# A two-layer MetaFormer on one core: padding cleared alone, qkv weights in thirds, ten convolution rows on VectorE, two dispatch steps a tap

## The chip, the cores and the metric

The kernel runs on one core of a Trainium2 chip, all in float32. The core has five instruction streams that run beside each other and meet only at semaphores: TensorE for matrix products (PE in the profile; PEld is its loading of weights), VectorE (DVE), ScalarE (ACT), GpSimd (POOL) and SyncE (SP, which here only starts transfers). Products land in PSUM banks, and another engine has to evict them. The metric is the device time of one execution in microseconds (us); lower is better. Before the change the median of three runs is 3289.18 us (3285.77 to 3293.74).

## The reference

The input is x with 4 images of 384 channels on 32x32 pixels. Two layers follow each other, each of the form "x plus mixer of norm(x), then plus feed-forward of norm(x)":

```python
# layer 0
x = x + conv0(ln_c(x))     # attention over the 1024 pixels, 8 heads of 48, with clipped relative
                           # tables for query, key and value; then a projection with bias
t = t + ffn0(ln_t(t))      # 384 -> 1536 -> 384, both weights Kronecker products, exact gelu
# layer 1
x = x + conv1(ln_c(x))     # depthwise 7x7 + 5x3 + 3x5 + (1x7 then 7x1) + (1x5 then 5x1) + bias
t = t + ffn1(ln_t(t))      # 4 experts of 384 -> 1536 -> 384, the best 2 of each token, weighted
```

ln_c and ln_t subtract the mean over channels and divide by the standard deviation. The depthwise kernels are summed into one 7x7 kernel, which fits since all are centered: 49 taps per channel.

## The kernel before

The work runs in three phases.

`qkv_phase` computes queries, keys and values for 8 tiles of 512 tokens. Channels lie on partitions in KC = 3 chunks of 128. For a tile, `token_stats` transposes the tokens (`row_ps`, line 75), takes mean and variance on VectorE (`s_st`, `s_mv`), and a square root on ScalarE gives `rstd`. The mean is not subtracted from x; instead `center` takes from the weight `wq` its mean over input channels (matmuls with a matrix of ones, `sum_ps`, line 116, then three VectorE operations on `wq` per 384 columns, line 118). `to_partitions` spreads `rstd` over partitions (`s_dg`, `all_ps`, lines 103 and 105). Six products `qk_ps` of three matmuls each follow (line 163), scaled by VectorE into `qk_sb`, then four `v_ps` products, scaled by ScalarE into `va` (line 177). `va` holds each head's 48 value columns padded to VW = 64; the padding must be zero, and line 135 clears the whole tile on GpSimd. That clearing stands on GpSimd's stream after the first half of `make_identity` (a clearing of `ident`) and ahead of its second half (the select that writes the diagonal). SP loads the first x tile, then `wq` in three row blocks of 576 KB, then the next two x tiles.

`attention_phase` handles the 8 heads in an order written out by hand. The change does not touch it.

`rest_phase` does everything after attention, image by image. `front(b)` is the attention's projection (`proj_ps`, line 903, its sum into the residual `xb` at line 906) and the whole first feed-forward; `normalise(b)` prepares the convolution, `image(b)` writes the padded picture `img`, `convolve(b)` runs the taps, and `dispatch(b)` is gates (`gate_ps`, `logits_ps`, eight transposed tiles `row_ps`, which VectorE takes for statistics and ScalarE copies into `rows`), then positions and expert block lists on VectorE (`pos`, `slot`, `row`) and 16 scatters of token rows into `xs_d` on GpSimd (line 1103). All of these are generators: a `yield` ends a step and gives an estimate of what the step costs VectorE and PE.

The expert part runs in 67 blocks of 128 tokens, in four groups of 13, 16, 16 and 22; group b needs the scatters of images up to b. In `blocks` each block gathers its tokens (`xg`, line 1147, GpSimd), transposes them (`xT_ps`, line 1160), and makes twelve times three `e_ps` matmuls (line 1198), a gelu on ScalarE and one `y_ps` matmul (line 1176). Weights come by indirect DMA on GpSimd (line 1166), three half blocks ahead; where the expert stays the same, the transfer moves nothing. `yo` (line 1179) evicts a block's sum on VectorE. After every twelfth of a block `more` adds 1.36 to PE's clock of estimates and takes steps from `others()` until VectorE's clock of estimates has caught up. So the remaining convolutions, fronts and dispatches are woven into the blocks by these estimates. At a group's end a loop, whatever the clocks say, takes steps until the next group's scatters are issued:

```python
for i, g in enumerate(groups):
    blocks(g, lambda k: more(g, k))
    if i + 1 < len(groups):
        while "after" not in groups[i + 1]:
            next(todo)
```

Image 0's convolution comes before all blocks, in `first()`, and is split between two engines. VectorE takes all of chunk 0 and the first `own` = 4 rows of chunk 1, one `scalar_tensor_tensor` per tap and part (line 993). PE takes the rest by `taps_by_matmul`: chunk 2 in two parts of 16 rows and chunk 1's other 28 rows in two parts of 14, with diagonal weights in 64x64 quarters (`tap_ps`, line 1037), even and odd taps in two halves that ScalarE copies out (`taps`, line 1047) and one more matmul adds up (`taps_ps`, line 1048, a single bank). VectorE then adds the part to `xb` (line 1051). `taps_by_matmul` is a generator too, with 27 steps a part: 25 pairs of taps, the sum, the add. `first()` takes three of its steps after each tap of VectorE.

Within an engine's stream the Tile framework may move instructions by its own priorities; instructions wrapped in `tc.keep_in_program_order` keep their order among each other.

Of the kernel before, what the change touches and what calls it, by code (L numbers as in the profile page):

```python
# [13 lines left out]
ALU = mybir.AluOpType  # L14
# [4 lines left out]
P = 128  # L19
# [101 lines left out]
def qkv_phase(tc, cst, x, w_qkv, qk_d, v_d, xs_d):  # L121

    nc = tc.nc
    one, ident = cst["one"], cst["ident"]
    with ExitStack() as es:
        wp = es.enter_context(tc.tile_pool(name="q_w", bufs=1))
        work = es.enter_context(tc.tile_pool(name="q_work", bufs=2))  # L130
        ev = es.enter_context(tc.tile_pool(name="q_ev", bufs=4))
        psum = es.enter_context(tc.tile_pool(name="q_ps", bufs=3, space=PSUM))
        psmm = es.enter_context(tc.tile_pool(name="q_mm", bufs=4, space=PSUM))
        va = wp.tile([P, HEADS, B * NBLK, VW], F32, name="va")
        nc.gpsimd.memset(va, 0.0)
        zero = wp.tile([P, 1, C], F32, name="zero")
        nc.gpsimd.memset(zero, 0.0)
        wq = wp.tile([P, KC, 3 * C], F32, name="wq")
        xts = {}

        def load(t):
            b, n0 = divmod(t * TOK, N)
            xts[t] = work.tile([P, KC, TOK], F32, tag="xt", name="xt", bufs=3)
            nc.sync.dma_start(xts[t], x[b, :, n0 : n0 + TOK].rearrange("(k p) n -> p k n", p=P))

        load(0)
        for k in range(KC):
            nc.sync.dma_start(wq[:, k, :], w_qkv[k * P : (k + 1) * P, :])
        stats = result(token_stats(nc, (work, psum, "st"), ident, xts[0], cst["eps6"]))
        center(nc, psum, "st", one, wq)  # L150
        for t in range(NT // TOK):
            b, n0 = divmod(t * TOK, N)
            xt = xts.pop(t)
            _, rstd = stats
            ps = to_partitions(nc, (work, psum, "st"), ident, one, rstd)
            scale = work.tile([P, TOK], F32, tag="scale", name="scale")
            nc.scalar.copy(scale, ps)
            if t + 1 < NT // TOK:
                load(t + 1)
            for m in range(2 * KC):  # L160
                ps = psmm.tile([P, TOK], F32, tag="mm", name="qk_ps")
                for k in range(KC):
                    nc.tensor.matmul(  # L163
                        ps, wq[:, k, m * P : (m + 1) * P], xt[:, k, :], start=(k == 0), stop=(k == KC - 1)
                    )
                sb = ev.tile([P, TOK], F32, tag="qk", name="qk_sb")
                nc.vector.tensor_tensor(sb, ps, scale, ALU.mult)
                nc.gpsimd.dma_start(qk_d[m * P : (m + 1) * P, t * TOK : (t + 1) * TOK], sb)
            if t + 1 < NT // TOK:
                stats = result(token_stats(nc, (work, psum, "st"), ident, xts[t + 1], cst["eps6"]))  # L170
            for j in range(TOK // P):
                ps = psmm.tile([P, TOK], F32, tag="mm", name="v_ps")
                for k in range(KC):
                    nc.tensor.matmul(
                        ps[:, :C], xt[:, k, j * P : (j + 1) * P], wq[:, k, 2 * C :], start=(k == 0), stop=(k == KC - 1)
                    )
                nc.scalar.activation(  # L177
                    va[:, :, t * (TOK // P) + j, :HD], ps[:, :C].rearrange("p (h d) -> p h d", d=HD),
                    AF.Copy, scale=rstd[:, j, :],
                )  # L180
            w = NBLK // 2 * VW
            nc.gpsimd.dma_start(
                v_d.rearrange("h p n -> p h n")[:, :, t * w : (t + 1) * w],
                va[:, :, t * NBLK // 2 : (t + 1) * NBLK // 2, :].rearrange("p h c d -> p h (c d)"),
            )
            if 2 <= t < 2 + NEXP:
                rows = xs_d[(t - 2) * CAP : (t - 1) * CAP].rearrange("(n p) c -> p n c", p=P)
                n = rows.shape[1] // 2
                for r in (rows[:, :n], rows[:, n:]):
                    tc.keep_in_program_order(nc.gpsimd.dma_start(r, bcast(zero, 1, r.shape[1])))  # L190
# [644 lines left out]
def rest_phase(tc, cst, x, ao_d, ins, xs_d, y_d, x2_d, out):  # L835
# [9 lines left out]
    with ExitStack() as es:  # L845
# [138 lines left out]
        def convolve(b, xb, parts):  # L984


            for k in range(KC):
                nc.vector.tensor_scalar_add(xb[:, k, :], xb[:, k, :], cbias[:, k : k + 1])
            acc = xb.rearrange("p k (y x) -> p k y x", x=IMG)
            for dy in range(7):  # L990
                for dx in range(7):
                    for k, y0, y1 in parts:
                        nc.vector.scalar_tensor_tensor(  # L993
                            acc[:, k, y0:y1], img[:, k, dy + y0 : dy + y1, dx : dx + IMG],
                            w7[:, k, dy, dx : dx + 1], acc[:, k, y0:y1], ALU.mult, ALU.add,
                        )

                    if b:
                        tc.keep_in_program_order(nc.vector.memset(pause, 0.0))
                    yield sum(0.12 + 0.0337 * (y1 - y0) for _, y0, y1 in parts) + 0.06, 0.0  # L1000
            if b + 1 < B:
                nc.sync.dma_start(x2_d[:, b * N : (b + 1) * N].rearrange("(k p) n -> p k n", p=P), xb)
# [10 lines left out]
        def taps_by_matmul(xb, parts):  # L1013

            def diagonals(k, w):
                d = w[:, : 49 * 64].rearrange("p (t m) -> p t m", m=64)
                nc.gpsimd.tensor_tensor(
                    d, bcast(half.unsqueeze(1), 1, 49),  # L1020
                    bcast(w7[:, k].rearrange("p y x -> p (y x)").unsqueeze(2), 2, 64), ALU.mult,
                )
                return d

            half = small.tile([P, 64], F32, tag="half", name="half", bufs=1)
            nc.vector.tensor_tensor(half, ident[:, :64], ident[:, 64:], ALU.add)
            diag = {k: diagonals(k, w) for k, w in zip(dict.fromkeys(k for k, *_ in parts), wts[1])}
            yield
            for k, y0, ny in parts:
                n = ny * IMG  # L1030
                sums = [ps_y.tile([P, TOK], F32, tag="y", name="tap_ps", bufs=2) for _ in range(2)]
                for t0 in range(0, 49, 2):
                    for t in range(t0, min(t0 + 2, 49)):
                        dy, dx = divmod(t, 7)
                        for h in range(2):
                            lo = 64 * h
                            nc.tensor.matmul(
                                sums[h][64 * (t % 2) : 64 * (t % 2) + 64, :n].rearrange("p (y x) -> p y x", x=IMG),
                                diag[k][lo : lo + 64, t, :],
                                img[lo : lo + 64, k, dy + y0 : dy + y0 + ny, dx : dx + IMG],  # L1040
                                start=(t < 2), stop=(t > 46),
                            )
                    yield
                po = ps_y.tile([P, TOK], F32, tag="t", name="taps_ps")
                for h in range(2):
                    e = hid.tile([P, TOK], F32, tag="hs", name="taps", bufs=HS)
                    nc.scalar.copy(e[:, :n], sums[h][:, :n])
                    nc.tensor.matmul(po[64 * h : 64 * h + 64, :n], half, e[:, :n], start=True, stop=True)
                yield
                acc = xb[:, k, y0 * IMG : y0 * IMG + n]  # L1050
                nc.vector.tensor_tensor(acc, acc, po[:, :n], ALU.add)
                yield

        def new(shape, name, dt=F32):
# [226 lines left out]
        def first():  # L1281


            half, own = IMG // 2, 4
            rest = (IMG - own) // 2
            taps = taps_by_matmul(
                xbs[0], [(2, 0, half), (2, half, half), (1, own, rest), (1, own + rest, rest)]
# [2 lines left out]
            halves = []  # L1290
            yield from normalise(xbs[0], halves)
            yield from image(halves)
            for _ in convolve(0, xbs[0], [(0, 0, IMG), (1, 0, own)]):
                for _ in range(3):
                    next(taps, None)
                yield
            for _ in taps:
# [3 lines left out]
        def others():  # L1301
# [11 lines left out]
            for b in range(1, B):  # L1313
# [2 lines left out]
                halves = []  # L1316
                later = ahead(b + 1, halves)
                for t, cost in enumerate(convolve(b, xbs[b], [(k, 0, IMG) for k in range(KC)])):
                    for start, steps in ((2, side), (12, later)):
                        more = next(steps, None) if t >= start else None  # L1320
                        if more:
                            cost = cost[0] + more[0], cost[1] + more[1]
                    yield cost
# [150 lines left out]
```

## Time and profile before

| what | us |
|---|---|
| median of 3 runs | 3289.18 |
| profiled execution | 3284.5 |
| its span, first to last instruction | 3282.7 |
| PE busy | 2986.8 (91%) |
| VectorE busy | 1991.4 (61%) |
| first PE instruction | 15.02 |
| image 0's convolution, first tap matmul to last add | 1752.4 to 1859.0 |
| first expert matmul | about 1938 |
| last convolution tap | about 2596 |
| last expert block's transposes | 3232.7 |

Times in the timeline are counted from the span's start. A timeline line reads: start, duration, engine, source line, operation, output <- input, shapes, how many instructions were merged, and in square brackets how long the engine stood idle before and what released it. A line of a stretch gives the window, its length, then the busy time (and the number of instructions) of PE, PEld, DVE, ACT and POOL, the clock that PE was granted (1.00 is full), the share of the DMA engines and GB/s. A float32 matmul leaves two records.

### The profile page before, as it was taken

To read this page: it belongs to the slowest core of one execution; us is meant where nothing else is said; L and a number is where in the kernel's file an instruction comes from. 1 tells how busy PE (TensorE), PEld (TensorE's weight loads), DVE (VectorE), ACT (ScalarE), POOL (GpSimd) and SP (SyncE) were. 2 spreads that over 40 slices of the span, in tenths; PEclk is the share of its full clock that TensorE was granted. 3 is DMA by queue.
4 is the path that set the end of the run, shared out by engine and by line. 5 is a ranking of instruction groups with operands and counts; after the bars stand their busy time and mean duration, and the time that the engine had idled before them with its cause. 6 is when DMAs were issued, how large, how long until landed. Compare 5 with 4: busy or idle time off the path is not lost.

```text
span 3282.7 us, 64040 instructions
## 1 busy us (share of the span) xinstructions
PE 2986.8 (91%) x25591; PEld 2063.8 (63%) x25591; DVE 1991.4 (61%) x3619; ACT 1331.7 (41%) x2687; POOL 1159.6 (35%) x1100
## 2 busy tenths in 40 slices
PE   8998998989898989999879888998999999999996
PEld 4445666666675656666643445575577777777775
DVE  2227777768676877777748659998999730001101
ACT  1115656555555655565511131342443333233322
POOL 2225536263536364544520032123125231114422
PEclk9999999999999999999989998998999999999998
DMA  3786464545455555646240313261156035474852
GB/s 140 268 300 195 102 194 115 179 122 174 117 174 129 169 136 141 171 120 187 74 153 23 113 66 142 80 257 56 44 209 234 27 115 213 152 277 151 303 208 70
DMA packets 222202, 500.60 MB, mean 152 GB/s; under 512 B 92192, under 2 KB 145056, under 8 KB 214224
## 3 DMA queue, kind: packets, MB, share of 16 engines
q1 hardware_dynamic: 156720, 214.75, 21.4%
q0 software_dynamic: 43552, 228.24, 18.8%
q10 hardware_dynamic: 21632, 53.52, 6.4%
q8 instruction: 202, 3.31, 0.4%
q14 instruction: 96, 0.79, 0.1%
HBM read 543.58 MB, written 152.37 MB: 212 GB/s over the span
## 4 chain that ended last, share of the span: by engine, by line
PE 65%; DVE 12%; issue 8%; ACT 7%; DMA 5%; POOL 3%; SPq 1%; another core or an unknown queue 0%; ACTq 0%; POOLq 0%; DVEq 0%
PE e_ps L1198 14%; PE y_ps L1176 13%; DVE xb L993 7%; PE av_ps L215 6%; PE t_ps L406 6%; PE tabq_ps L215 5%; PE sc_ps L215 4%; PE tv_ps L215 3%; ACT arow L387 3%; PE tabk_ps L215 2%; PE qk_ps L163 2%; ACT aT L407 2%; PE a_ps L416 2%; DVE oT L470 2%; DMA qs<-qk_d 1%
## 5 line engine op out<-in xcount | busy, mean ns | idle before, releaser
L349 POOL TENSOR_TENSOR bias<-b,s 128x416 f32<-128x416 f32 (+24 forms) x656 | 660.0, 1043 | 631.8 <-DMA s<-sd 424.5
L1198 PEld LDWEIGHTS e_ps<-xT,w 128*128 128x128 f32 x4824 | 654.6, 192 | 230.5 <-issue 16.7
L1198 PE MATMUL e_ps<-xT,w 128*128 128x128 f32 x4824 | 672.6, 277 | 20.2 <-DVE xb L906 8.0
L1176 PE MATMUL y_ps<-w,eh 128*128 128x384 f32 x1608 | 652.5, 490 | 17.7 <-ACT eh L1201 14.3
L993 DVE SCALAR_TENSOR_TENSOR xb<-img,c_w,xb 128x1024 f32<-128x1024 f32 (+1 forms) x539 | 611.0, 1196 | 0.0
L1201 ACT ACTIVATE eh<-e_ps,w 128x128 f32<-128x128 f32 x804 | 293.3, 367 | 753.8 <-PE e_ps L1198 692.3
L1166 POOL DMA_INDIRECT w<-in_w,row x134 | 164.0, 1224 | 786.4 <-PE y_ps L1176 270.7
L377 DVE CUSTOM_DVE_ANT_0 arow<-sc_ps,bias 128x1024 f32<-128x1024 f32 x256 | 312.8, 1222 | 191.4 <-POOL bias L349 101.9
L398 DVE TENSOR_REDUCE extra<-arow 128x32 f32<-128x32 f32 (+24 forms) x768 | 378.7, 551 | 30.2 <-ACT arow L387 30.2
L406 PEld LDWEIGHTS t_ps<-ident,arow 128*128 128x128 f32 x2048 | 226.4, 144 | 265.0 <-ACT arow L387 185.3
L407 ACT COPY aT<-t_ps 128x512 f32<-128x512 f32 x512 | 275.5, 589 | 267.4 <-PE t_ps L406 241.9
L387 ACT ACTIVATE arow<-arow,nm 128x1024 f32<-128x1024 f32 x256 | 297.0, 1160 | 177.6 <-DVE nm L377 166.5
L406 PE MATMUL t_ps<-ident,arow 128*128 128x128 f32 x2048 | 289.1, 286 | 74.4 <-ACT arow L387 73.3
L215 PE MATMUL sc_ps<-kk,qs 48*32 48x512 f32 x4096 | 294.0, 625 | 50.8 <-DMA qs<-qk_d 26.8
L1179 DVE TENSOR_TENSOR yo<-y_ps,w 128x384 f32<-128x384 f32 x67 | 37.2, 556 | 446.9 <-PE y_ps L1176 439.7
L1176 PEld LDWEIGHTS y_ps<-w,eh 128*128 128x128 f32 x1608 | 248.0, 193 | 31.1 <-ACT eh L1201 16.9
L215 PEld LDWEIGHTS av_ps<-aT,vb 128*64 128x64 f32 x4096 | 222.3, 137 | 52.3 <-ACT aT L407 37.8
L303 DVE STREAM_TRANSPOSE b<-tabk_ps 128x480 f32<-128x480 f32 x256 | 219.1, 1000 | 44.5 <-PE tabk_ps L215 24.8
L215 PE MATMUL av_ps<-aT,vb 128*64 128x128 f32 x4096 | 237.7, 274 | 0.0
L215 PE MATMUL tabk_ps<-tab,kq 48*128 48x480 f32 x512 | 225.7, 588 | 3.3 <-DVE b L303 3.3
L215 PE MATMUL tabq_ps<-tab,kq 48*128 48x480 f32 x512 | 224.5, 585 | 0.7 <-ACT va L177 0.7
L308 ACT COPY st<-tabq_ps 128x480 f32<-128x480 f32 x256 | 141.8, 561 | 75.3 <-PE tabk_ps L215 36.5
(212 smaller groups left out, 3190.4 us busy)
## 6 DMA issues: line engine op xcount, KB each, us to landing
sd<-st SPq DMA_DIRECT2D x128, 480.0 KB
s<-sd SPq DMA_DIRECT2D x512, 120.0 KB
xs_d<-zero POOLq DMA_DIRECT2D x8, 3072.0 KB
tvw<-in_tv ACTq DMA_DIRECT2D x120, 192.0 KB
y_d<-yo SPq DMA_DIRECT2D x67, 192.0 KB
qk_d<-qk_sb POOLq DMA_DIRECT2D x48, 256.0 KB
qs<-qk_d SPq DMA_DIRECT2D x256, 48.0 KB
kq<-qk_d ACTq DMA_DIRECT2D x56, 192.0 KB
```

The lines of the kernel that those rows point to most:

```text
L215: ins = nc.tensor.matmul(*args, **kw)
L303: turn = nc.vector.transpose(b2.rearrange("p e y x -> p x (e y)")[:, i + j], ps[:, j, : SPAN * IMG])
L349: nc.gpsimd.tensor_tensor(bias[:, y0:y1, :], bass.AP(b2.tensor, b2.offset + (e * IMG + y0) * IMG, [list(b2.ap[0]), [(step * IMG + 1) * IMG ...
L377: nc.vector.tensor_tensor_reduce(s["flat"], ps.rearrange("p h n -> p (h n)"), s["bias"].rearrange("p y x -> p (y x)"), -SCALE, BIG, ALU.ad ...
L387: nc.scalar.activation(s["flat"], s["flat"], AF.Exp, bias=s["nm"], scale=-1.0, accum_out=dn[:, y % YT : y % YT + 1])
L398: pin(nc.vector.tensor_reduce(ex[:, i, :], a[:, p0:p1, :].rearrange("p y x -> p x y"), AX.X, ALU.add))
L406: pin(nc.tensor.transpose(pt[:, j, :], s["flat"][:, k0 : k0 + P], ident))
L407: pin(nc.scalar.copy(aT[:, 4 * g : 4 * g + 4, s["y"] % YB, :], pt))
L993: nc.vector.scalar_tensor_tensor(acc[:, k, y0:y1], img[:, k, dy + y0 : dy + y1, dx : dx + IMG], w7[:, k, dy, dx : dx + 1], acc[:, k, y0:y1 ...
L1176: nc.tensor.matmul(py, hs, w[:, o : o + C], start=(ff == 0), stop=(ff == NF - 1))
L1198: nc.tensor.matmul(ph, w[:, o : o + P], xT[k][:, c, :], start=(c == 0), stop=(c == KC - 1))
L1201: nc.scalar.activation(hs, ph, AF.Gelu, bias=w[:, o : o + 1])
```

## The change

There are three separate edits.

At the start, only the padding columns of `va` are cleared, on VectorE. `wq` is loaded in nine pieces of 192 KB, first the query third of all three row blocks, then the key third, then the value third; and each third is centered right before its first use: the query third before product 0, the key third before product 3 and the value third before the first `v_ps`, all in tile 0.

In image 0's convolution VectorE takes ten rows of chunk 1 instead of four, and PE two parts of 11 rows instead of 14. The taps of image 0 and the adds of line 1051 are kept in program order. The 108 steps of `taps_by_matmul` are spread over the taps from the third to the last, the rest at the last, so an add stands after every twelfth tap or so: after taps 13, 25, 37 and 48 (counted from 0).

In `others()` each tap of images 2 and 3 takes two steps of the dispatch of the image before, instead of one, from the third tap on; the next image's front still joins with one step per tap from the thirteenth.

```diff
         va = wp.tile([P, HEADS, B * NBLK, VW], F32, name="va")
-        nc.gpsimd.memset(va, 0.0)
+        nc.vector.memset(va[:, :, :, HD:], 0.0)
...
         load(0)
-        for k in range(KC):
-            nc.sync.dma_start(wq[:, k, :], w_qkv[k * P : (k + 1) * P, :])
+
+        for i in range(3):
+            for k in range(KC):
+                own = slice(i * C, (i + 1) * C)
+                nc.sync.dma_start(wq[:, k, own], w_qkv[k * P : (k + 1) * P, own])
         stats = result(token_stats(nc, (work, psum, "st"), ident, xts[0], cst["eps6"]))
-        center(nc, psum, "st", one, wq)
...
             for m in range(2 * KC):
+                if t == 0 and m % KC == 0:
+                    center(nc, psum, "st", one, wq[:, :, m * P : m * P + C])
...
+            if t == 0:
+                center(nc, psum, "st", one, wq[:, :, 2 * C :])
             for j in range(TOK // P):
...
                     for k, y0, y1 in parts:
-                        nc.vector.scalar_tensor_tensor(
+                        tap = nc.vector.scalar_tensor_tensor(
                             acc[:, k, y0:y1], img[:, k, dy + y0 : dy + y1, dx : dx + IMG],
                             w7[:, k, dy, dx : dx + 1], acc[:, k, y0:y1], ALU.mult, ALU.add,
                         )
+                        if b == 0:
+                            tc.keep_in_program_order(tap)
...
                 acc = xb[:, k, y0 * IMG : y0 * IMG + n]
-                nc.vector.tensor_tensor(acc, acc, po[:, :n], ALU.add)
+                tc.keep_in_program_order(nc.vector.tensor_tensor(acc, acc, po[:, :n], ALU.add))
...
-            half, own = IMG // 2, 4
+            half, own = IMG // 2, 10
...
-            for _ in convolve(0, xbs[0], [(0, 0, IMG), (1, 0, own)]):
-                for _ in range(3):
+
+            steps = 4 * 27
+            for t, _ in enumerate(convolve(0, xbs[0], [(0, 0, IMG), (1, 0, own)])):
+                for _ in range(steps if t == 48 else max(0, t - 1) * steps // 48 - max(0, t - 2) * steps // 48):
                     next(taps, None)
                 yield
...
-                    for start, steps in ((2, side), (12, later)):
+                    for start, steps in ((2, side), (2, side), (12, later)):
                         more = next(steps, None) if t >= start else None
```

## The prediction

> **What bounds the kernel now.** I read the page first, then the stretches of 50 us, then the timeline where TensorE (PE) is not full, and the chain of waits there. The page:
>
> ```profile
> PE 2986.8 (91%) x25591; PEld 2063.8 (63%) x25591; DVE 1991.4 (61%) x3619; ACT 1331.7 (41%) x2687; POOL 1159.6 (35%) x1100
> PE 65%; DVE 12%; issue 8%; ACT 7%; DMA 5%; POOL 3%; SPq 1%; another core or an unknown queue 0%; ACTq 0%; POOLq 0%; DVEq 0%
> ```
>
> PE is busy 91% of the span and carries 65% of the chain that ended last, so a change pays where it takes away idle time of PE, or work that PE stands behind. The stretches (busy us of PE, PEld, DVE, ACT, POOL, then PE clock):
>
> ```profile
> 1800.00:1850.00 50.00, 41.87 (x380) 18.78 (x376) 33.39 (x47) 2.04 (x4) 0.00 (x0) 0.90 0.14 52
> 2000.00:2050.00 50.00, 34.56 (x127) 21.37 (x126) 47.08 (x63) 7.26 (x15) 7.44 (x4) 0.76 0.44 166
> 2250.00:2300.00 50.00, 35.76 (x148) 22.44 (x147) 41.64 (x62) 11.64 (x21) 19.71 (x17) 0.83 0.15 49
> 2700.00:2750.00 50.00, 50.00 (x311) 39.97 (x310) 1.67 (x3) 15.04 (x40) 9.40 (x10) 1.00 0.65 239
> ```
>
> From 2700 on PE is full: there every microsecond won earlier reaches the end. The change touches three places with holes: the start, image 0's convolution (1752 to 1859), and the border between block groups 0 and 1 (2245 to 2300). At the start (timeline):
>
> ```profile
> 0.89 13.76 POOL L135 MEMSET va<- 128x16384 f32 x1
> 14.69 0.28 POOL masks.py:199 TENSOR_SCALAR_AFFINE_SELECT ident<-ident 128x128 f32<-128x128 f32 x1
> 15.02 2.82 PE L75 MATMUL row_ps<-ident,xt 128*128 128x128 f32 x12 [15.02 <-POOL ident masks.py:199]
> 17.64 6.87 PE L116 MATMUL sum_ps<-wq,one 128*128 128x384 f32 x18
> 25.20 15.61 PE L163 MATMUL qk_ps<-xt,wq 128*128 128x512 f32 x36
> ```
>
> PE's first instruction waits 15.02 us for the identity, which stands behind the va memset on POOL. In image 0's convolution:
>
> ```profile
> 1806.20 19.31 PE L1037 MATMUL tap_ps<-img,w 64*64 64x448 f32 x196
> 1832.91 1.76 PE L1048 MATMUL taps_ps<-taps,half 128*64 128x448 f32 x4 [7.41 <-DVE xb L1051]
> 1834.60 21.34 PE L1037 MATMUL tap_ps<-img,w 64*64 64x448 f32 x196
> 1858.33 0.62 DVE L1051 TENSOR_TENSOR xb<-xb,taps_ps 128x448 f32<-128x448 f32 x1 [22.99 <-PE taps_ps L1048]
> ```
>
> PE ends last; VectorE (DVE) then idles 23 us. Besides, PE waits 7.4 us for an add that stands late in DVE's stream, and its next 20 tap matmuls run at half pace. At the group border:
>
> ```profile
> 2236.86 1.02 POOL L1103 DMA_INDIRECT xs_d<-rows,pos  x1 [21.77 <-DVE b_first L782]
> 2261.81 1.02 POOL L1147 DMA_INDIRECT xg<-xs_d,slot  x1 [1.01 <-DMA xs_d<-rows,pos]
> 2265.04 0.88 PE L1160 MATMUL xT_ps<-ident,xg 128*128 128x128 f32 x3 [7.52 <-DMA xg<-xs_d,slot]
> ```
>
> Group 1's first gather waits for the 16 scatters of image 1, and these for the positions, which come late from DVE.
>
> **A, the start.** POOL loses a 13.76 us memset; DVE gets one of 128x4096. DVE's memsets give 0.17 us for 128 elements and 0.06 for 2, about 0.9 ns each, so 3.6 us, done by about 5 us and hidden under the load of xt. PE then starts when xt lands. No row shows that: of a 768 KB load issued at 1663.31 PE had the data at 1670.09 (6.8 us, beside other loads), and a 192 KB gather took 3.1 us. So PE starts between 3.9 and 9 us; I take 7, nearer the 768 KB row. SP issues nine DMAs instead of three, at 0.54 us (1.63 for three): 3.3 us more ahead of xt's next two loads, which PE needs 18 us after its start; covered.
>
> "DMA: Bandwidth & Descriptors" in the Trainium skill (section Measured) speaks against this split: it asks for transfers of 1 MiB or more, and its anatomy section puts about 2.0 us plus bytes/436 GB/s on each. No row shows these nine; the 16 scatters here, issued 1.3 us apart, land 2.6 us after their issue, so they overlap. By the page's figures xt lands at an estimated 4.5 us and the q third, in series, at 11.9, 1.2 later than PE would ask for it; A would then be worth 15.0 - 4.5 - 4.9 - 1.2 = 4.4 us, and 5.6 if they overlap.
>
> Against that PE's order gets worse. The first all_ps now precedes the sums and needs the rstd chain (transposes to s_dg took 5.0 us here): 2.2 us of idle. The q third is centered before its products (0.3), the k third between (0.6, after six transposes), the next tile's all_ps waits for statistics that nothing covers now (1.3), the v third 0.3. With 0.2 of slow clock that is 4.9 us. **A = 15.0 - 7 - 4.9 = 3.1 us gained.** The ends of the start give 6.2 and 1.1; with up to 2 more of waiting for the k third, whose centering shares DVE with three evictions, -1.
>
> **B, ten rows on DVE.** Per tap DVE gets 192 elements more. Pairs took 40.57 us for 55 taps, 1.475 a pair; a 1024 tap alone takes 1.20 (3.60 for three in image 1), so the 128 one 0.27 and an element 1.04 ns: 0.20 more, 1.675 a pair, 82.1 for 49. PE: 512 columns took 22.0 us, 448 took 19.3, so 352 take 15.3, twice. The adds are now pinned after taps 13, 25, 37 and 48. PE's first part ends 1782 as before; its second sum is ready at 1806.2, DVE comes to that add at 1803.8 and waits 2.4. Parts three and four end at 1823 and 1840.6, and no PE wait for an add is left (DVE is there at 1827, PE needs the bank at 1839). DVE: 1760.0 + 82.1 + adds 0.60 + 0.60 + 0.47 + wait 2.4 + last add 0.5 = 1846.7, against 1858.95: 12.2 less. What is late next is DVE. PE idles 4.7 us before the gate products and then runs slow for a few us (after the 7.4 us idle five steps took 0.75 instead of 0.38): 2 back. If 352 columns run no faster than 448, PE ends at 1850 and 8 are left. **B = 10; bounds 7 and 12.** All that follows up to group 0's tenth block has the same order on every engine, so it shifts whole, with its 15 us hole at 2009 to 2031.
>
> **C, two dispatch steps a tap.** This moves only dispatch 1 and 2 (image 1's and 2's gates, positions, scatters). In the built stream of DVE the positions of image 1 now come 61.7 taps into the convolutions instead of 65.0: 3.3 x 3.65 = 12.0 us earlier, 2224.6 on the old clock. POOL's 16 scatters took 22.6, so they end at 2247.2; a weight fetch goes first, and the gather lands 5.3 us later (2259.8 to 2265.0 before), at 2252.5. PE comes to the border at 2244.7 and some 0.8: it still waits 7, then runs slow (2.5, as from 2265 to 2272).
>
> What goes is more. The forced loop at the border no longer pulls image 3's projection into it; that now stands 0.67 blocks (10.5 us) later in PE's stream and DVE is there first. Before, PE idled 18.1 of the 167.8 us from 2244.7 to image 2's gates (position 18.42 of 67 blocks), at clock 0.95: about 4 more. In the new order the gates stand at 19.67, with 1.25 blocks (20 us of PE) more done by then. PE reaches the projection at 2252.5 + 3 + 10.5 = 2266 and needs 153 us from there (6 blocks of 15.7, six transposes of 0.45, image 3's front 56): 2419. DVE starts on it when the first sum is there, 2268.6, and took 165.4 with 9.7 idle; one tap less and little idle make 154 to 157: 2424, against 2411.7 + 20 = 2431.7. Gain 8. From it: eight transposed tiles now pass three PSUM buffers within two taps (1 us for dispatch 2, since DVE took such tiles 1 us after PE wrote them at 2187), and POOL has 14 scatters in a row (18 us) between two weight fetches whose slack is 21: 1.5 in the mean, 5 if late for real weights. **C = 5.5; bounds -3 (bunches of 3 each, a late fetch of 5, half the gain) and 13 (no wait at the border).**
>
> On the other queues only places change: on SP one y_d store trades places with two xb loads (about 0.3 us each, their data is needed tens of us later); the table loads of ACT (1.28 us each) go with the gates, as many as before.
>
> **Sum.** 3.1 + 10 + 5.5 = 18.6. The profiled execution took 3284.5 us (span 3282.7, 1.8 around it), so 3265.9; the median of the runs shown is 4.7 above it, so 3271.
>
> **The rivals.**
> 1. C pays nothing, because DVE bounds the stretch from 2250 to 2425 anyway (it was busy 159.4 of 167.8 us): only A and B, 13 gained, less up to 6 for C's new waits: 3276 to 3282. For it: DVE's 95%. Against: its idle of 8.4 us was PE's wait at the border.
> 2. The border's wait goes entirely and xt lands early: 6 + 12 + 13 = 31, 3258.
> 3. Slower: the bunched gates. If PE runs ahead of DVE by two to three taps when it writes those tiles, it stands as at 2009 to 2031, where it did 7.6 us of work in 22.5 at clock 0.58 behind adds late on DVE: up to 17 us at dispatch 1 and 17 at 2. 34 lost against 18.6 won is 15 slower, 3305; it decides from 9.3 us lost at each. For it: the three buffers. Against: the 1 us at 2187.
> 4. The start doesn't move or loses (xt late) and the 352 columns run no faster: with C at nothing 5 is left, no change.
>
> **How the numbers follow.** A measurement of this kernel can tell about 0.2%, 6.6 us. Forecast (13 to 25 gained) 0.58; first rival 0.20; second 0.09; so faster 0.87. Fourth, and mixtures that leave less than 6.6 either way, 0.07 the same. Third 0.06 slower. The sums of all low and high bounds are 3 and 31 gained; the range takes 5 to 32 with the scatter of the runs: 3257 to 3284.
>
> **What would show it.** A: PE's first row at about 7 us, the qk products of tile 1 near 47 instead of 50.1. B: the last L1051 add 12 us nearer the first tap and waiting little; no PE wait for DVE at L1048; a PE hole of 5 us before gate_ps. C: positions and scatters 12 us earlier, the wait on xg at the first gather at 7 or less, and 2250 to 2300 above 40 us busy. I am wrong if xt lands after 10 us, if the 320-element tap takes over 0.5 us, or if row_ps transposes show waits of several us on DVE s_st around the two dispatches.

## The result and the profile after

The change makes no difference that can be measured: 3286.82 us in the median of four runs (3285.9 to 3288.1) against 3287.47 for the kernel before beside it; the ratio is 1.0, with a 95% interval from 0.9977 to 1.0022. Forecast were 3271 us and a gain. The profiled execution took 3287.29 us (span 3285.5), where that of before took 3284.5 (span 3282.7).

The page of the changed kernel, engines and shares of the chain that ended last (lines of the functions moved by 6 to 10):

```profile
PE 2985.8 (91%) x25591; PEld 2068.8 (63%) x25591; DVE 2004.9 (61%) x3620; ACT 1332.4 (41%) x2687; POOL 1148.4 (35%) x1099
PE 60%; DVE 12%; ACT 6%; issue 5%; DMA 5%; POOL 3%; SPq 1%; another core or an unknown queue 1%; ACTq 0%; POOLq 0%; DVEq 0%
```

PE is busy for as long as before to a microsecond, and the span is 2.8 longer, so what was won in one place was given back in another. The start of the changed kernel (timeline):

```profile
1.83 3.47 DVE L135 MEMSET va<- 128x4096 f32 x1 [0.80 <-issue]
5.46 2.79 PE L75 MATMUL row_ps<-ident,xt 128*128 128x128 f32 x12 [5.46 <-DMA xt<-in_x]
10.65 2.05 PE L105 MATMUL all_ps<-s_dg,one 128*128 128x512 f32 x2 [2.39 <-DVE s_dg L103]
12.49 5.38 PE L116 MATMUL sum_ps<-wq,one 128*128 128x384 f32 x10
17.71 7.89 PE L167 MATMUL qk_ps<-xt,wq 128*128 128x512 f32 x18
```

PE starts 9.6 us earlier and waits for xt alone. By the first `qk_ps` 7.5 us are left of that (17.71 against 25.20), and by the first matmul of attention 3.1 (234.1 against 237.2). Image 0's convolution, PE's rows and then VectorE's:

```profile
1804.88 15.24 PE L1045 MATMUL tap_ps<-img,w 64*64 64x352 f32 x196
1837.62 1.17 PE L1056 MATMUL taps_ps<-taps,half 128*64 128x352 f32 x4 [0.59 <-ACT taps L1055]
1843.84 5.33 PE L608 MATMUL gate_ps<-xb,c_gate_w 128*32 128x512 f32 x12 [5.05 <-DVE xb L999]
```
```profile
1825.49 0.52 DVE L1059 TENSOR_TENSOR xb<-xb,taps_ps 128x352 f32<-128x352 f32 x1
1844.17 0.51 DVE L1059 TENSOR_TENSOR xb<-xb,taps_ps 128x352 f32<-128x352 f32 x1
```

Now VectorE ends last: its last add is at 1844.17 instead of 1858.33, no add of PE's parts is waited for, and PE stands 5.05 us before the gates and then takes 5.33 for products that take 2.77 in the later images (the granted clock is 0.54 from 1843 to 1850). The border between block groups 0 and 1:

```profile
2215.02 1.96 POOL L1111 DMA_INDIRECT xs_d<-rows,pos  x1 [7.16 <-DVE b_first L788]
...
2241.19 1.05 POOL L1174 DMA_INDIRECT w<-in_w,row  x1 [0.30 <-issue]
2243.24 1.30 POOL L1155 DMA_INDIRECT xg<-xs_d,slot  x1 [1.00 <-DMA xs_d<-rows,pos]
...
2246.75 0.87 PE L1168 MATMUL xT_ps<-ident,xg 128*128 128x128 f32 x3 [10.69 <-DMA xg<-xs_d,slot]
```

The scatters begin 21.8 us earlier than before, and the gather follows 18.6 earlier, but PE waits 10.69 us where it waited 7.52. The stretches of 50 us (columns as in the prediction):

```profile
1800.00:1850.00 50.00, 43.04 (x446) 22.32 (x438) 43.92 (x56) 3.39 (x8) 0.00 (x0) 0.93 0.35 135
2200.00:2250.00 50.00, 38.74 (x228) 30.54 (x227) 49.74 (x116) 10.48 (x29) 28.88 (x23) 0.89 0.22 80
2250.00:2300.00 50.00, 49.48 (x238) 33.51 (x237) 36.45 (x56) 13.90 (x30) 8.28 (x7) 0.98 0.07 21
2650.00:2700.00 50.00, 40.26 (x222) 31.65 (x221) 17.54 (x126) 10.56 (x29) 20.94 (x21) 0.85 0.31 114
```

The hole of 2250 to 2300 (35.76 us of PE before) has moved into 2200 to 2250, and 2650 to 2700, where PE was nearly full, now has a hole of 10. The same two stretches in the kernel before:

```profile
2200.00:2250.00 50.00, 49.08 (x280) 37.06 (x279) 49.57 (x136) 22.79 (x49) 12.40 (x12) 1.00 0.32 124
2650.00:2700.00 50.00, 48.64 (x299) 38.72 (x298) 9.64 (x58) 14.60 (x40) 12.72 (x13) 1.00 0.25 91
```

The second hole is the dispatch of image 3, which the prediction does not price. ScalarE's waits there, first in the kernel before from 2590 to 2690, then in the changed one:

```profile
ACT eh L1201 <- issue: 7.3, 2, 6.1
```
```profile
ACT eh L1209 <- remote: 14.6, 3, 8.8
ACT eh L1209 <- issue: 2.9, 2, 2.0
```

A line reads: what waited, what ended it, us in total, times, longest. "issue" says that nothing in the profile ended the wait, "remote" that what ended it is no instruction or transfer that the profile shows. The gelu `eh` comes late, and PE's `y_ps` with it. In the changed kernel the three "remote" ones lie between 2655 and 2671, while GpSimd issues 13 scatters in a row; VectorE's instructions of 0.2 us then stand up to a microsecond apart too.

To place such losses, the time at which VectorE starts to evict each block's sum (`yo`) is taken from the timeline. us between blocks, in the kernel before, the changed one and its experiments; blocks are counted from 0, and each column is one profiled execution, good to about 0.1 us:

| from, to | what lies in it | before | after | e5: all | e7: image 2 | e8: A, B, spread | e1: A, B | e2: C |
|---|---|---|---|---|---|---|---|---|
| first tap matmul, block 0 | convolution, dispatch 0 | 223.9 | 213.2 | 215.4 | 215.1 | 215.1 | 200.5 | 212.0 |
| 8, 12 | image 1's gates | 71.0 | 72.9 | 72.9 | 70.9 | 70.9 | 71.0 | 73.0 |
| 12, 17 | border, image 3's front | 162.7 | 160.5 | 160.8 | 163.4 | 163.6 | 163.7 | 160.8 |
| 17, 22 | image 2's gates | 90.6 | 91.4 | 91.3 | 99.2 | 90.5 | 90.5 | 91.4 |
| 22, 23 | a weight fetch | 16.1 | 18.5 | 18.6 | 16.1 | 16.1 | 16.1 | 18.5 |
| 23, 29 | image 3's taps | 96.4 | 97.9 | 97.9 | 97.5 | 96.4 | 96.4 | 97.9 |
| 29, 32 | image 3's dispatch | 71.4 | 79.0 | 78.2 | 72.6 | 64.7 | 64.8 | 65.9 |
| 0, 66 | all blocks | 1274.1 | 1288.0 | 1285.9 | 1285.9 | 1269.0 | 1261.1 | 1265.7 |

In the changed kernel block 0 is 10.5 us early, and the blocks take 13.9 longer: block 66 is 3.4 late.

### The profile page after: what moved, and what is told of

Same layout as the page of the kernel before. It is cut to its first block, busy times and chain, and to the rows that moved or that the text cites. A ratio compares the mean times of both kernels' runs of the same rounds, so it can differ in the third digit from the quotient of the medians.

```text
span 3285.5 us, 64033 instructions
## 1 busy us (share of the span) xinstructions
PE 2985.8 (91%) x25591; PEld 2068.8 (63%) x25591; DVE 2004.9 (61%) x3620; ACT 1332.4 (41%) x2687; POOL 1148.4 (35%) x1099
## 4 chain that ended last, share of the span: by engine, by line
PE 60%; DVE 12%; ACT 6%; issue 5%; DMA 5%; POOL 3%; SPq 1%; another core or an unknown queue 1%; ACTq 0%; POOLq 0%; DVEq 0%
PE e_ps L1206 13%; PE y_ps L1184 13%; DVE xb L999 6%; PE av_ps L221 6%; PE t_ps L412 5%; PE tabq_ps L221 5%; PE sc_ps L221 4%; PE tv_ps L221 3%; ACT arow L393 2%; PE tabk_ps L221 2%; ACT aT L413 2%; PE a_ps L422 2%; DVE oT L476 2%; DMA qs<-qk_d 1%; PE tap_ps L1045 1%
## 5 line engine op out<-in xcount | busy, mean ns | idle before, releaser
L1206 PEld LDWEIGHTS e_ps<-xT,w 128*128 128x128 f32 x4824 | 658.0, 193 | 239.7 <-issue 18.6
L999 DVE SCALAR_TENSOR_TENSOR xb<-img,c_w,xb 128x1024 f32<-128x1024 f32 (+1 forms) x539 | 619.9, 1210 | 0.0
L221 PE MATMUL tabq_ps<-tab,kq 48*128 48x480 f32 x512 | 223.9, 584 | 0.7 <-ACT va L183 0.7
```

The costliest lines, as they stand in the source:

```text
L221: ins = nc.tensor.matmul(*args, **kw)
L999: tap = nc.vector.scalar_tensor_tensor(acc[:, k, y0:y1], img[:, k, dy + y0 : dy + y1, dx : dx + IMG], w7[:, k, dy, dx : dx + 1], acc[:, k, ...
L1206: nc.tensor.matmul(ph, w[:, o : o + P], xT[k][:, c, :], start=(c == 0), stop=(c == KC - 1))
```

## The experiments

The experiments ran on three chips, and the times differ between them: on the chip of e1 to e4 the kernel before took 3260 us, on that of e9 to e15 3258 and 3259, on that of e5 to e8 3290. Which chip the first pair ran on is not on record; its 3287 is like the last. So each kernel is compared with the kernel before on its own chip, by the medians, with the interval of the ratio. The kernels of e1 to e15 share the lines of the changed kernel unless a diff shows otherwise.

**Each part alone (e1 to e4).** e1 is the changed kernel without C:

```diff
-                    for start, steps in ((2, side), (2, side), (12, later)):
+                    for start, steps in ((2, side), (12, later)):
```

> The start (A) and the ten rows (B) as changed, one dispatch step a tap as before. The order of every engine in the expert blocks is then that of the kernel before. Theory (C takes back what B won): block 0's sum is evicted about 10.5 us earlier than before (1965.8 against 1976.3), and block 66's too (3240 against 3250.4); the time is 9 to 11 below the kernel before, about 3277. Rival (the earlier start is lost to anything that the expert blocks wait for, weights or transfers, whatever the dispatch steps do): block 66 at 3250 or later and the time as before. If A's 3 us were to survive attention, 13 less.

Measured: 3247.08 against 3260.23, 13.2 less (ratio 0.9958, 0.9946 to 0.997). The blocks take 1261.1 us, as with A alone (e4, 1260.7): without C they give nothing back on this chip.

e2 is the opposite edit on the kernel before.

> Only the two dispatch steps a tap, on top of the kernel before. Theory (C takes back what B won): block 0 as before (1976), at block 23 some 3 later than before, after image 3's dispatch (block 32) 12 later, at block 66 some 14 later: time 12 to 15 above the kernel before, about 3300. Rival (the blocks lose only because they start earlier): the time as before, within 3. The forecast's own C would be 5.5 below.

Measured: 3263.65, 3.4 more (1.0008, 0.9999 to 1.0016). Its blocks take 1265.7 us, against 1260.7 with A alone (e4) on the same chip, so C costs 5 there, not 14: the theory has the sign right and the size wrong. By the time alone, whose interval holds no change, it could not be told from the rival. Image 3's dispatch lost nearly nothing on this chip (65.9 against 64.8).

e3 undoes A and C, e4 undoes B and C.

> Only the ten rows on VectorE with their pinned order. Theory: block 0's sum 10.5 earlier, the same at block 66, time 9 to 11 below the kernel before. Rival (the blocks take it back): as before.

Measured: 3248.3, 11.9 less (0.9962, 0.9949 to 0.9975).

> Only the start: the padding cleared alone on VectorE and the weights in thirds. Theory (attention loses it again in waits for loads of qs): the first attention matmul 3 us earlier (234 against 237), the first projection at 1670 as before, time as before within 2. Rival (the late wait in the profile of after was one execution's): projection at 1667, time 3 below.

Measured: 3255.82, 4.4 less (0.9989, 0.998 to 0.9998). The first attention matmul stands at 232.6 and the first projection at 1667.2, so the rival holds here. Attention itself scatters: over all twelve profiles with A its first matmul stands at 230.9 to 235.1 (mean 232.8), over the five without at 236.4 to 238.5 (237.4); the first projection at 1663.1 to 1675.3 (1669.2) and 1666.8 to 1674.5 (1670.5). A brings 4.6 us to attention; from there to the projection single executions vary by about six either way, which hides it, in the first pair of profiles wholly (PE's waits for loads of `qs` between 1480 and 1672 are 2.0 before and 5.2 after).

**Why the whole change gains nothing (e5 to e8).** e5 is the changed kernel again. In e6 and e7 one image's dispatch alone takes two steps, for e6:

```diff
-                    for start, steps in ((2, side), (2, side), (12, later)):
+                    for start, steps in ((2, side), (2 if b == 2 else 99, side), (12, later)):
```

and `b == 3` for e7. e8 is e1 with image 3's scatters and the weight fetches of blocks 30 to 39 held in program order and the pause between the pairs of scatters, which counts on VectorE's clock of estimates, set from 2.6 to 8:

```diff
             scattered.append(ins_)
+            if len(scattered) > 48:
+                tc.keep_in_program_order(ins_)
...
+                if 30 <= g["start"] + k < 40:
+                    tc.keep_in_program_order(load)
...
-            side = dispatch(b, 0.0 if b + 1 < B else 2.6)
+            side = dispatch(b, 0.0 if b + 1 < B else 8.0)
```

> The whole change again, A, B and C, on the chip of the variants beside it. Theory: A and B win 13 where C costs 5 in the blocks and up to 9 more where ScalarE and VectorE stand still during image 3's scatters: on a chip where the kernel before takes about 3260 the dispatch of image 3 runs without standing still and the time is 7 to 9 below the kernel before; on a chip where it takes about 3287 the time is that of the kernel before, within 3. Rival (C takes back all of A and B on every chip): as before within 3 on either.

Measured: 3287.18 against 3289.74, 2.6 less (0.9992, 0.9981 to 1.0003), as the theory has it for this chip, though the rival's bound of 3 holds as well.

> A and B, and two dispatch steps a tap for image 1's dispatch alone; image 2's keeps one. The border loop, the projection of image 3 and the dispatch of image 3 stand where they stand in the changed kernel, but image 2's dispatch is spread over eight taps again. Theory: against A and B alone 1 to 3 lost (image 1's gates 1.8, border 2.8 won, late image 3 dispatch 1 to 9 by chip); no wait on a weight transfer in the blocks 20 to 24. Rival (image 1's bunch costs most of C): 5 or more lost by block 13.

Measured: 3273.19, 16.5 less (0.9948, 0.9935 to 0.9961), with no wait for weights (16.1 from block 22 to 23), image 1's part at 72.9 and image 3's dispatch, now with 10 scatters in a row, at 75.7. So one step a tap for image 2 alone brings 14 of what the whole change lacks in the medians (6 of them show in the blocks of the profiled execution, 1279.5 against 1285.9; it was the longest of its five, and where the other 8 went is not shown). The loss against A and B alone, of which the theory speaks, can't be read here, since A and B alone did not run on this chip.

> A and B, and two dispatch steps a tap for image 2's dispatch alone. Border and projection stand as before the change, and so does image 3's dispatch. Theory: against A and B alone 2 to 5 lost, between blocks 18 and 24, 3 of them one wait of PE for a weight transfer queued on GpSimd behind ten scatters. Rival (late weights come from where the blocks stand, not from the bunch): nothing lost.

Measured: 3281.81, 7.9 less (0.9975, 0.9961 to 0.9988); from block 17 to 22 it takes 99.2 us instead of 90.6, so 8.6 are lost there, more than the theory's 2 to 5. GpSimd's rows and PE's wait in e7:

```profile
2441.99 2.00 POOL L1111 DMA_INDIRECT xs_d<-rows,pos  x1 [1.16 <-DVE b_first L788]
...
2457.95 0.97 POOL L1111 DMA_INDIRECT xs_d<-rows,pos  x1 [0.31 <-issue]
2459.23 2.10 POOL L1174 DMA_INDIRECT w<-in_w,row  x1 [0.30 <-issue]
```
```profile
PE e_ps L1206 <- DMA w<-in_w,row: 7.5, 2, 5.8
```

Ten scatters take 17 us, the weight fetch behind them is late, and the next one again behind six more. The whole change has one such wait of 3.0 us, behind 14 (e2 and e10 have it too).

> A and B with one step a tap, and image 3's 16 scatters put two by two between the weight fetches (in the kernel before eleven and five in a row). Theory (ScalarE and VectorE stand still for as long as GpSimd issues scatters in a row, and PE waits for the gelu): the dispatch of image 3 (blocks 29 to 32) falls from 65 to 71 us to 58 to 62; 3 to 10 less than A and B alone, most on a chip where the kernel before takes about 3287. Rival (the stand-still is not from the scatters): blocks 29 to 32 as with A and B alone, same time.

Measured: 3267.45, 22.3 less (0.9927, 0.9915 to 0.994). On the same chip PE's waits during image 3's dispatch, in e5 and then in e8:

```profile
PE y_ps L1184 <- issue: 6.9, 1, 6.9
PE y_ps L1184 <- ACT eh L1209: 6.0, 3, 3.0
PE before_ps L702 <- DVE mask L656: 1.6, 1, 1.6
```
```profile
PE y_ps L1188 <- ACT eh L1213: 4.0, 3, 2.1
```

Blocks 29 to 32 take 78.2 us in e5 (13 scatters in a row), 72.6 in e7 (11 and 5, as in the kernel before) and 64.7 in e8 (two by two). The last is not the 58 to 62 that the theory had; it is what the other chips take (e1 64.8 with 11 and 5, e2 65.9 with 13). So on this chip breaking up the row of scatters ends the standing still of ScalarE and PE. The edit of e8 also pins the weight fetches; this was not tried apart from the scatters.

**The spread on its own, and a best version (e9 to e15).** e9 and e13 are e1 again, e14 is e8 again. e10 is the changed kernel with the spread of e8, e11 and e15 the kernel before with it, e12 is e6 with it. All ran on one further chip, which shows no standing still, so what their expectations say of a chip of about 3287 was not tried.

> A and B with one step a tap once more, beside kernels that differ from it in one thing each. Theory: 10 to 13 below the kernel before; blocks 0 to 66 as long as before (1261 where image 3's dispatch runs freely, about 1274 where ScalarE stands still in it). Rival (the 13 won came from another clock or a better run): less than 7.

Measured: 3245.11 against 3257.61, 12.5 less (0.9957, 0.9943 to 0.9971).

> A, B and C, with image 3's scatters put two by two between the weight fetches. Theory: what C loses in image 3's dispatch goes (blocks 29 to 32 at 64 to 66), what it loses at images 1 and 2 stays: 3 to 5 above A and B with the scatters spread, so 5 to 8 below the kernel before on a chip where it takes about 3260 and 16 to 19 below where it takes about 3287. Rival (C's late dispatch costs by its place, not by the run of scatters): blocks 29 to 32 still at 75 or more where the kernel before takes about 3287.

Measured: 3251.16, 6.5 less (0.9977, 0.9967 to 0.9987): this is 6 above A and B on the same chip, in the blocks 6.7 (1267.8 against 1261.1). Beside A and B with the spread (e14, 1262.6) the blocks are 5.3 longer, and that is C's share. The rival, a late dispatch that costs by its place where things stand still, was not put to the test on this chip.

> The kernel before with nothing changed but image 3's scatters, two by two between the weight fetches. Theory: 29 to 32 falls by 6.5, and the time by 6 to 9, where the kernel before takes about 3287; nothing where it takes about 3260. Rival (the gain of the spread version belongs to A and B): nothing on either.

Measured: 3260.86, 3.2 more (1.0009, 0.9997 to 1.002): nothing gained, as expected of a chip where nothing stands still.

> A and B, two steps a tap for image 1's dispatch alone, and image 3's scatters spread. Theory: border and image 1 together win 1 to 2 against A and B with the scatters spread, since image 2's weights are no longer late: 12 to 16 below the kernel before where it takes about 3260, 22 to 26 where it takes about 3287, the fastest so far. Rival (the border wins nothing): as A and B with the scatters spread.

Measured: 3248.52, 9.1 less (0.997, 0.996 to 0.9979): the theory fails. The border wins 4.4 from block 12 to 17 (159.4 against 163.8) and 1.5 are won from 17 to 22, but the gates of image 1 cost 2.0, blocks 23 to 32 4.6, and the rest of the blocks some 2 more; A and B alone are faster.

> A and B, one step a tap. Theory: 10 to 16 below the kernel before on any chip, since the order of the blocks is that of before; blocks 29 to 32 take 65 where the kernel before takes about 3260 and 71 to 73 where it takes about 3287. Rival (where ScalarE stands still the earlier start of the blocks is lost again): less than 6 below where the kernel before takes about 3287.

Measured: 3240.85 against 3258.81, 18.0 less (0.9953, 0.9939 to 0.9966). The ratio stands for 15; the median of these five runs lies near their lowest.

> A and B with image 3's scatters two by two between the weight fetches. Theory: blocks 29 to 32 at 64.7 on any chip; the time 6 to 8 below A and B alone where the kernel before takes about 3287, equal to it within 3 where it takes about 3260. Rival (the 22 won were not from the spread): as A and B alone on either.

Measured: 3244.35, 14.5 less (0.996, 0.9946 to 0.9973), as A and B alone within the scatter.

> The kernel before with image 3's scatters two by two. Theory: 6 to 8 below the kernel before where that takes about 3287, the same within 3 where it takes about 3260. Rival: the same on either.

Measured: 3260.0, 1.2 more (1.0003, 0.9994 to 1.0012).

A and B without C thus beat the kernel before on two chips, by 12 to 18 us in the medians and 0.4 to 0.5% in the ratios; the changed kernel as it stands was not timed on these two. With the spread they beat both kernels on the third, by 22 where the whole change gained 3. How much of the 22 A and B alone would keep there was not timed.

## Why the prediction was wrong

**A, forecast 3.1 gained.** Right in size. xt landed at 5.46 where 7 was taken, so PE's first row is 1.5 earlier; the loss in PE's order, forecast 4.9, was 5 to 6.5 by the start of attention: the wait for `s_dg` is 2.39 (2.2 forecast), but `all_ps` and most of the five sums run at about half pace, 2.05 and 5.38 us, where 0.2 of slow clock had been allowed. The granted clock reads 1.00 there, so what slowed them is not shown. What remains is 3.1 in the first profile, 4.6 in the mean of twelve, 4.4 in the time of A alone. The page "DMA: Bandwidth & Descriptors" of the Trainium skill (its anatomy section) led to an estimate of 4.5 us for xt, and the measured 5.46 is nearer to it than to the 7 taken from a row. But that section gives its price for transfers that GpSimd issues, and xt is issued by SyncE: one load that lands near the estimate does not show that the price holds there. For the nine pieces of `wq`, against which the prediction set the same page, PE has no wait in the changed kernel: in the first 60 us its only waits are 5.5 for xt and 3.1 for `s_dg`.

**B, forecast 10.** Right, with two errors that nearly cancel. The 352 columns take 15.24 us (15.3 forecast) and the hole before the gates is 5.05 (4.7). The last add ends 92.0 us after the first tap where the forecast had 94.3, mostly since VectorE waits 0.9 for PE's second sum and not 2.4: 14.5 won at this place instead of 12.2. But 3.8 of it are gone by block 0, where 2 had been taken back; the gate products alone cost 2.6. From the first tap to block 0 the gain is 10.7 in the first pair and 11 to 12 on the other chips, 11.9 in the time of B alone.

**C, forecast 5.5 gained, with -3 as its low bound.** This is the step that failed, in three terms of its sum.

The border's gain of 8 was the largest and measured 2.2 (162.7 to 160.5; 2.8 and 4.4 on the other chips). VectorE was earlier, as forecast: the first scatter is at 2215.02, 11.3 us earlier on the clock of the blocks (that is, with the 10.5 us added by which block 0 is early), where 12 were forecast. But the 16 scatters took 25.9 us there, not the 22.6 that the prediction carried over: each took 1.33 us in the mean, where those of image 3, issued when no tap is left, take 0.99. So the gather landed at 2257.3 on this clock, 4.8 later than the 2252.5 forecast.

PE came to the border at 2246.6 and waited 10.69 instead of 7, and the first sum of image 3's projection, from which the forecast counted VectorE's way to image 2's gates, stood at 2272.7 instead of 2268.6. For that way the forecast had 154 to 157 us and it took 159.5, with VectorE idle for only 3.4. (The prediction reads 165.4 with 9.7 idle for it in the kernel before; from the sum at 2248.1 to the gates at 2411.7 it is 163.6 with 8.4.) So image 2's gates come at 2432.2 where 2424 was forecast, half of the 8 through the late sum, half on VectorE's longer way; 2431.7 would have been no gain, and the 2.2 less what the two bunches cost (1.9 and 0.8, below) is the -0.5 that is left.

The bunches: image 1's gates cost 1.9 (the 1 of the forecast was for image 2's, which cost 0.8). The late weight fetch, named in the prediction at 1.5 in the mean and 5 if late, was late: 3.0 in PE's wait, 2.4 from block 22 to 23. Blocks 23 to 29 lose 1.5 more without a wait that the trace shows.

Left out altogether was image 3's dispatch. C does not name it, but the border's loop had taken steps without charging them to VectorE's clock of estimates; when it takes fewer, everything later is charged and moves. In PE's stream image 2's gates go from block 18.42 to 19.67, which the prediction has, and image 3's from 30.33 to 31.58, and with them the scatters: 13 in a row in place of 11. In e6, where image 1's dispatch alone is bunched, both move as far, in e7 neither does. On the chip of e1 and e2 that costs a microsecond (64.8 to 65.9). On the chip of the first pair it costs 7.6, the largest single loss (71.4 to 79.0; 78.2 in e5). What standing still adds to blocks 29 to 32, against a chip without it, goes with the length of the row: 6.6 and 7.8 with 11 scatters in a row (before and e7 against e1), 7.7 with 10 (e6 with 75.7, against the 68.0 of e12, where they are spread), 13.1 and 12.3 with 13 (after and e5 against e2). So most of the 7.6 is put down to the longer row and a microsecond to the later place; the two were not tried apart on one chip.

The terms measured: 2.2 - 1.9 - 0.8 - 2.4 - 1.5 - 7.6 = -12.0, and -1.9 in the later and first blocks make the 13.9 of the table. The bound of -3 left room for half a gain and one late fetch, not for a dispatch outside the change. Without the standing still C is about 5 us of loss in the blocks (e2 against e4, e10 against e14).

**The rivals.** The outcome is that of the fourth, no change, by another way: neither the start nor the 352 columns failed. The first (VectorE bounds the stretch behind the border, C pays nothing) had the border nearest to right. The third named the bunched gates as the mechanism of a loss; they cost 2 us, not the 9.3 from which it would have decided, and no transposed tile waits for VectorE there (from 2160 to 2200 and from 2415 to 2445 PE waits for `eh` alone). The chances of 0.87 for faster rested on A and B alone bringing 13, which they do; what was underrated is that one part could take all of it back. That it came out at just nothing is partly the chip: the 7.6 of image 3's dispatch were a microsecond on the chip of e2.

What stays open: what makes ScalarE and VectorE stand still. No instruction or transfer of the trace ends these waits, and two of three chips do not show them. That they go when the rows of scatters are broken up is shown by e5, e7 and e8; how the scatters bring them on is not, and the changed kernel with its scatters spread did not run on a chip that shows them.

## What to carry to other kernels

Where estimates decide the order, list every group of instructions that changes place, and price each, above all those that the edit does not name: here the dispatch of image 3 cost more (7.6 us) than the two that were edited. A queue that serves both bulk scatters and just-in-time fetches should carry them mixed; ten or more in a row made a fetch late in e7 and, on one chip of three, went with other engines standing still in e5. And price parts by themselves: A and B were right, and a version without C is the better kernel (e8 on the chip of e5, by 20 us, with the scatters spread).

## What the runs showed that was not expected

The same program differs by 0.9% between chips. From the first tap to block 0 the chip of the first pair needs 223.9 us where the others need 212.0 (e2) with the same code, from block 29 to 32 71.4 and 64.8, from block 50 to 52 37.8 and 33.5. All three hold rows of indirect transfers: in the last, eight gathers of expert results go out in a row, and it stays at 38.2 in e8, which spreads image 3's scatters alone. In the first, 16 scatters go out in a row and ScalarE waits for nothing that the profile names; the lines are ScalarE's waits in the changed kernel from 1840 to 1980, and e1 and e2 have no such line there:

```profile
ACT o L954 <- issue: 7.2, 1, 7.2
ACT hs L950 <- remote: 3.6, 1, 3.6
```

A gain or a loss of a few microseconds that rests on such a place belongs to the chip as much as to the kernel, and needs runs on more than one.
